# The row tiles of the pairs transposed by VectorE and five transfers instead of by TensorE

## The chip, the cores and the metric

One Trainium2 chip (trn2), one NeuronCore of it. The metric is the device time of one execution in microseconds. The engines are called PE (TensorE; PEld is its weight load), DVE (VectorE), ACT (ScalarE), POOL (GpSimd) and SP (SyncE, which here only issues transfers). Each engine works through its own list of instructions in order; semaphores make one wait for another.

## The reference

The input x has 2048 rows of 1024 numbers, in fp32 as everything here. A first layer is a linear map whose weight is a product of two matrices under a sparse mask, then gelu, the residual sum and a LayerNorm. A second layer is a linear map whose weights are looked up from packed codes in a table of 16 entries (or of 256, where a row's norm is over 64, which the kernel checks and leaves to a general path that isn't run here), again with residual sum and LayerNorm.

```python
def _L0_attn_ref(x, w1, w2, b2, sparse_mask):
    attn = jnp.einsum('ds,td->st', w1, w2) * sparse_mask
    y = jnp.einsum('bds,st->bdt', x, attn) + b2
    return jax.nn.gelu(y, approximate=False)

def _L0_ffn_ref(x, qweight, lut4, lut8, bias):
    e = jnp.linalg.norm(x, axis=-1) * LIN_SLOPE + LIN_INTER
    mask = e > EST_T
    w_l = dequant_kbit(qweight, lut4, B_L)
    w_h = dequant_kbit(qweight, lut8, B_H)
    y_l = jnp.einsum('bsi,oi->bso', x, w_l)
    y_h = jnp.einsum('bsi,oi->bso', x, w_h)
    y = jnp.where(mask[..., None], y_h, y_l) + bias
    return y

x = _layernorm(x + _L0_attn_ref(x, ...), axis=-1)
x = _layernorm(x + _L0_ffn_ref(x, ...), axis=-1)
```

## The kernel before

The rows are cut into 16 tiles of 128 (`NT`), each kept in SBUF as `x_tiles[n]` of 128x1024. PE contracts over partitions, so every row tile has to be there transposed, as 8 blocks of 128x128, before it can be multiplied.

First the two weights are made: `attn`, the masked product, as a band (L416, L423), and `wT`, the table weights, which the generator behind `steps()` unpacks piece by piece on DVE, POOL and ACT (L273 to L314) and PE transposes. The identity is added to `wT`, so the residual of the second layer is in the product.

Then the list `todo` (L625 to L632) is worked off. An entry "attention" transposes a tile on PE (`transpose_columns`, L258, copied from PSUM by ACT in L259), multiplies it with the band (L462), and goes through bias (DVE L477), gelu (ACT L478), residual sum (DVE L480) and LayerNorm. "left" and "right" are the two halves of 512 columns of the second layer for the tiles 0 to 5 (`EARLY` of them); the transposed tile is kept in the buffers `early0` to `early5` between the two. `ffn_half` ends in `combine` (DVE L502), and for the right half in `finish_rows`. A LayerNorm is: `nm` from the row sum (DVE L346), the sum of squares (ACT L349), the inverse root (POOL L351, L352) and `normalize` (DVE L356), into `o` and a transfer out for the second layer. The last twelve entries alternate right 0, attention 10, right 1, attention 11 and so on to right 5, attention 15. Two PSUM tiles `mm` of two banks each take turns, so a right half waits for the `combine` of the right half before, and an attention sum for the `z` read (L477) of the attention before.

The tiles 6 to 15 are done as five pairs. `pair_inputs` and `ffn_pair` multiply a pair's two row tiles as a 2x2 block product with seven products instead of eight, on sums of blocks: `weight_sums` makes t1 to t4 of the weights once (DVE L539 to L542), `pair_inputs` makes the blocks a11, a12, a22 and the sums s1 to s4 of a pair's transposed rows. A product is four matmuls of 128x128 by 128x512 (`times`, L582). PSUM holds u (twice), v and w for it, in the banks that `mm` had. Between the products DVE empties the sums: y11 (L595), y22 (L597), y12 (L599), then four `combine`, of which the last of each tile leads to `finish_rows`.

In `pair_inputs` PE makes four groups of four transposes (L556); a group takes every eighth column of its tile, as `wT` has them in that order. ACT copies three groups out of PSUM (L563, L564, L569), DVE makes s1 and s3 (L566, L567) reading the PSUM group of a21, and POOL makes s2 and s4 (L568, L570). Its results lie in `early0` to `early5` again, three of them for each pair, with two sets taking turns, and in `a22`. `pair_inputs` of the next pair is called ahead of `ffn_pair` of this one (L681 to L686), so its transposes stand in PE's list just ahead of this pair's products. A tile scheduler puts the instructions of each engine into an order by its own estimate, keeping dependences; so the order in the program text isn't quite the order on the engines. `count_odd` (L611) counts the rows that would need the general path, behind the first pair.

Of the kernel before, what the change touches and what calls it, by code (L numbers as in the profile page):

```python
# [9 lines left out]
FP = mybir.dt.float32  # L10
# [4 lines left out]
ALU = mybir.AluOpType  # L15
AX = mybir.AxisListType

P = 128
D = 1024
SOON = 12  # L20
PAIR = 2
KT = D // P
HALF = 512
# [4 lines left out]
WORDS = D // 32  # L28
BAND = 70
WIN = P + 2 * BAND  # L30
EARLY = 6
AHEAD = 2


def window(s):

    return max(0, s * P - BAND), min(D, (s + 1) * P + BAND)
# [153 lines left out]
def kernel(  # L191
# [13 lines left out]
    nc = tc.nc  # L205
    x = x.flatten_outer_dims()
    out = out.flatten_outer_dims()
    NT = x.shape[0] // P
# [4 lines left out]
    with ExitStack() as main:  # L213
        const = main.enter_context(tc.tile_pool(name="const", bufs=1))
        ps_tr = main.enter_context(tc.tile_pool(name="ps_tr", bufs=4, space=bass.MemoryType.PSUM))
# [5 lines left out]
        dq = first_sb.enter_context(tc.tile_pool(name="dq", bufs=1, side="right"))  # L221
        xp0 = main.enter_context(tc.tile_pool(name="xp0", bufs=1))
        work = main.enter_context(tc.tile_pool(name="work", bufs=1))


        q = dq.tile([P, KT, B_L, WORDS], I32, name="q")
# [11 lines left out]
        ident = const.tile([P, P], FP, name="ident")  # L238
# [119 lines left out]
        x_tiles = []  # L358
# [5 lines left out]

        attn = band.tile([P, KT, WIN], FP, name="attn")


        with tc.tile_pool(name="prod", bufs=1) as prod:
# [8 lines left out]
            def load_w1(first, n):  # L377
# [32 lines left out]
            for s in range(KT):  # L410
# [88 lines left out]

        def combine(n, h, ps, other):  # L500

            nc.vector.scalar_tensor_tensor(  # L502
                x_tiles[n][:, ts(h, HALF)],
                ps,
                1.0,
                other,
                ALU.mult,
                ALU.add,
                accum_out=sums[:, n, h : h + 1],
            )  # L510
# [20 lines left out]
        KH = KT // 2  # L531
# [10 lines left out]
            nc.vector.tensor_tensor(t4, b21, t2, ALU.subtract)  # L542
            return t1, t2, t3, t4

        def pair_inputs(pool, n):


            def halves(tag):
                both = late.tile([P, KT, P], FP, tag=tag, name="halves")
                return both[:, :KH, :], both[:, KH:, :]  # L550

            def transposes(m, half):
                cols = x_tiles[m].rearrange("t (b s) -> t s b", s=8)
                pt = ps_tr.tile([P, HALF // P, P], FP, tag="tr", name="pt")
                for k in range(KH):
                    nc.tensor.transpose(pt[:, k, :], cols[:, half * KH + k, :], ident)  # L556
                return pt


            side = n // PAIR % 2  # L560
            (a11, a12), (s1, s2), (s3, s4) = (halves(f"early{2 * i + side}") for i in range(3))
            a22 = pool.tile([P, KH, P], FP, tag="a22", name="a22", bufs=2)
            nc.scalar.copy(a11, transposes(n, 0))  # L563
            nc.scalar.copy(a22, transposes(n + 1, 1))  # L564
            a21 = transposes(n + 1, 0)
            nc.vector.tensor_tensor(s1, a21, a22, ALU.add)  # L566
            nc.vector.tensor_tensor(s3, a11, a21, ALU.subtract)  # L567
            nc.gpsimd.tensor_tensor(s2, s1, a11, ALU.subtract)  # L568
            nc.scalar.copy(a12, transposes(n, 1))  # L569
            nc.gpsimd.tensor_tensor(s4, a12, s2, ALU.subtract)  # L570
            return a11, a12, a22, s1, s2, s3, s4

        def ffn_pair(pool, n, blocks, weights):
            a11, a12, a22, s1, s2, s3, s4 = blocks
            t1, t2, t3, t4 = weights
            u = pool.tile([P, HALF], FP, tag="u", name="u", bufs=2)
            v = pool.tile([P, HALF], FP, tag="v", name="v", bufs=1)
            w = pool.tile([P, HALF], FP, tag="w", name="w", bufs=1)

            def times(ps, a, b, start, stop):  # L580
                for k in range(KH):
                    nc.tensor.matmul(  # L582
                        out=ps,
                        lhsT=a[:, k, :],
                        rhs=b[:, k, :],
                        start=start and k == 0,
                        stop=stop and k == KH - 1,
                        skip_group_check=True,
                    )

            left, right = bias_bc[:, :HALF], bias_bc[:, HALF:]
            y11, y12 = x_tiles[n][:, :HALF], x_tiles[n][:, HALF:]
            y22 = x_tiles[n + 1][:, HALF:]
            times(u, a11, b11, True, False)
            nc.vector.tensor_tensor(y11, u, left, ALU.add)  # L595
            times(w, s1, t1, True, False)
            nc.vector.tensor_tensor(y22, w, right, ALU.add)  # L597
            times(u, s2, t2, False, False)
            nc.vector.tensor_tensor(y12, u, right, ALU.add)  # L599
            times(w, s4, b22, False, True)  # L600
            combine(n, 1, w, y12)
            times(u, s3, t3, False, False)
            combine(n + 1, 1, u, y22)
            times(v, a12, b21, True, True)
            combine(n, 0, v, y11)
            finish_rows(n)
            times(u, a22, t4, False, True)
            combine(n + 1, 0, u, left)
            finish_rows(n + 1)
# [15 lines left out]
        todo = [("attention", n) for n in range(4)]  # L625
        for m in range(EARLY):
            todo.append(("left", m))
            if m < 4:
                todo.append(("attention", 4 + m))
        todo += [("attention", 8), ("attention", 9)]  # L630
        for m in range(EARLY):
            todo += [("right", m), ("attention", 10 + m)]  # L632
        unpack_after = [("attention", 1), ("left", 0), ("attention", 4), ("left", 1)]
        unpack_after += [("attention", 6), ("left", 2), ("left", 3), ("left", 4)]

        kept = {}

        def prepare(what, n):
            if what == "attention":
                return transposed(n, "xT", 2, False)  # L640
            if what == "left":
                kept[n] = transposed(n, f"early{n}", 1, True)
            return kept[n]
# [3 lines left out]
        for i, (what, n) in enumerate(todo):  # L647
            if (what, n) == ("right", 0):
                steps(100)
                transpose_pending(0)  # L650
                first_sb.close()
                last = main.enter_context(tc.tile_pool(name="last", bufs=1, side="right"))
                for m in range(SOON, NT):
                    load_x(last, m)
            if (what, n) == ("left", 0):
                transpose_pending(0)
            xT = ready
            if i + 1 < len(todo):
                ready = prepare(*todo[i + 1])
            if what == "attention":  # L660
                attention(n, xT)
                if n > 8 and checks < KT:
                    check_outside(checks)
                    checks += 1
            else:
                ffn_half(n, xT, 0 if what == "left" else 1)
                if what == "left" and n > 1:
                    check_outside(checks)
                    checks += 1
                if (what, n) == ("right", 0):  # L670
                    weights = weight_sums(last)
            if (what, n) in unpack_after:
                steps(1)
        while checks < KT:
            check_outside(checks)
            checks += 1
        first_ps.close()
        ps_pair = main.enter_context(
            tc.tile_pool(name="ps_pair", bufs=1, space=bass.MemoryType.PSUM)
        )  # L680
        blocks = pair_inputs(last, EARLY)  # L681
        for n in range(EARLY, NT, PAIR):
            now = blocks
            if n + PAIR < NT:
                blocks = pair_inputs(last, n + PAIR)
            ffn_pair(ps_pair, n, now, weights)  # L686
            if n == EARLY:
                count_odd()

# [41 lines left out]
```

## Time and profile before

| | |
|---|---|
| median of 3 runs | 384.45 us (384.4 to 384.62) |
| the profiled execution | 384.95 us, span 383.2 us, mean PE clock 0.981 |
| PE busy | 341.1 us (89%) |
| DVE, ACT, POOL busy | 213.0, 149.0, 120.7 us |
| a matmul of the pairs (L582) | 592 ns a record, 8 records (4 matmuls) for a product |
| a transpose of the pairs (L556) | x80, 10.1 us busy, 279 ns |
| s1, s3 on DVE (L566, L567) | 690 and 678 ns |
| s2, s4 on POOL (L568, L570) | 1275 and 1439 ns |
| normalize into o (DVE L356) | 988 ns mean |
| a 512 KB transfer out | 2.6 us from issue to landing |

The profile is of one execution. Its span runs from the first to the last instruction; the execution's own time is 1.75 us longer. A group of instructions is given as line, engine, operation, what is written and read, and count. "[idle before <-X]" says how long the engine stood idle just ahead of an instruction and what ended that. The chain that ended last is followed back from the last instruction, at each step to what released it. Matmul records of PE overlap by their pipelining, so their starts say more than their sums.

### The profile page before, as it was taken

To read this page: it belongs to the slowest core of one execution; us is meant where nothing else is said; L and a number is where in the kernel's file an instruction comes from. 1 tells how busy PE (TensorE), PEld (TensorE's weight loads), DVE (VectorE), ACT (ScalarE), POOL (GpSimd) and SP (SyncE) were. 2 spreads that over 40 slices of the span, in tenths; PEclk is the share of its full clock that TensorE was granted. 3 is DMA by queue.
4 is the path that set the end of the run, shared out by engine and by line. 5 is a ranking of instruction groups with operands and counts; after the bars stand their busy time and mean duration, and the time that the engine had idled before them with its cause. 6 is when DMAs were issued, how large, how long until landed. Compare 5 with 4: busy or idle time off the path is not lost.

```text
span 383.2 us, 3726 instructions
## 1 busy us (share of the span) xinstructions
PE 341.1 (89%) x1306; PEld 213.3 (56%) x1306; DVE 213.0 (56%) x334; ACT 149.0 (39%) x233; POOL 120.7 (31%) x144
## 2 busy tenths in 40 slices
PE   3699775979989889979999999899999999999990
PEld 3587565875666465665566665534544545444430
DVE  2698798988968893059544355642521614314221
ACT  0952843986395366152355533600401203002011
POOL 1991871875274611012022212530400301201000
PEclk9999998989999999999999999999999999999995
DMA  9999005800010111034121211100110201101102
GB/s 223 350 353 301 37 3 196 352 2 0 0 46 1 40 41 42 0 120 142 65 86 66 76 55 55 56 0 1 55 56 0 109 0 54 57 0 57 52 3 115
DMA packets 19705, 31.31 MB, mean 82 GB/s; under 512 B 6624, under 2 KB 13536, under 8 KB 19680
## 3 DMA queue, kind: packets, MB, share of 16 engines
q1 hardware_dynamic: 14416, 30.41, 21.8%
q10 hardware_dynamic: 5264, 0.59, 1.1%
q8 instruction: 12, 0.20, 0.2%
q14 instruction: 13, 0.11, 0.1%
HBM read 22.61 MB, written 8.39 MB: 81 GB/s over the span
## 4 chain that ended last, share of the span: by engine, by line
PE 38%; DVE 26%; POOL 14%; ACT 10%; issue 7%; DMA 3%; ACTq 0%; POOLq 0%; DVEq 0%; SPq 0%
PE u L582 16%; PE w L582 8%; ACT junk L349 6%; POOL root L302 5%; PE v L582 4%; PE mm L490 4%; DVE root L307 4%; PE mm L462 3%; DVE x L480 3%; DVE root L306 3%; POOL r L352 3%; DVE root L311 3%; POOL e L302 2%; DVE e L305 2%; DVE z L477 2%
## 5 line engine op out<-in xcount | busy, mean ns | idle before, releaser
L349 ACT ACTIVATE junk<-x,nm 128x1024 bf16<-128x1024 f32 x32 | 36.8, 1150 | 140.5 <-DVE nm L346 140.5
L490 PE MATMUL mm<-wT,xT 128*128 128x512 f32 x192 | 84.8, 594 | 5.6 <-DVE x L502 2.7
L351 POOL TENSOR_SCALAR r<-ss 128x1 f32<-128x1 f32 x32 | 9.9, 310 | 203.1 <-ACT junk L349 202.6
L462 PE MATMUL mm<-attn,xT 128*128 128x198 f32 (+2 forms) x320 | 62.5, 352 | 5.3 <-ACT xT L259 5.3
L462 PEld LDWEIGHTS mm<-attn,xT 128*128 128x128 f32 x320 | 54.8, 197 | 13.7 <-ACT xT L259 5.7
L490 PEld LDWEIGHTS mm<-wT,xT 128*128 128x128 f32 x192 | 35.5, 190 | 46.8 <-issue 39.5
L298 ACT ACTIVATE e<-v,lt,diff 128x1024 f32<-128x1024 uint8 x32 | 38.3, 1242 | 11.9 <-DVE v L273 10.3
L302 POOL TENSOR_SCALAR root<-v,diff,lt 128x1024 f32<-128x1024 uint8 x16 | 38.9, 2434 | 8.1 <-DVE root L311 7.4
L302 POOL TENSOR_SCALAR e<-v,diff,lt 128x1024 f32<-128x1024 uint8 x16 | 28.7, 1795 | 28.6 <-DVE v L273 25.6
L582 PE MATMUL u<-t,halves 128*128 128x512 f32 x80 | 36.0, 593 | 0.9 <-DVE x L595 0.9
L356 DVE TENSOR_SCALAR o<-x,nm,r 128x1024 f32<-128x1024 f32 x16 | 15.8, 988 | 35.1 <-POOL r L352 35.1
L416 PE MATMUL mm<-w2T,w_sb 128*128 128x268 f32 (+1 forms) x128 | 29.5, 384 | 4.6 <-issue 2.8
L478 ACT ACTIVATE z<-z 128x1024 f32<-128x1024 f32 x16 | 16.9, 1055 | 32.0 <-DVE z L477 32.0
L259 ACT COPY xT<-pt 128x512 f32<-128x512 f32 x44 | 23.4, 581 | 14.9 <-PE pt L258 9.6
L416 PEld LDWEIGHTS mm<-w2T,w_sb 128*128 128x128 f32 x128 | 23.8, 196 | 8.7 <-issue 3.2
L258 PE MATMUL pt<-ident,x 128*128 128x128 f32 x176 | 23.7, 280 | 4.1 <-DVE x L356 2.3
L356 DVE TENSOR_SCALAR x<-x,nm,r 128x1024 f32<-128x1024 f32 x16 | 13.0, 813 | 25.5 <-POOL r L352 23.2
L306 DVE COPY_PREDICATED root<-v,e 128x1024 f32<-128x1024 uint8 x16 | 22.7, 1419 | 7.8 <-POOL root L302 7.8
L582 PEld LDWEIGHTS u<-t,halves 128*128 128x128 f32 x80 | 15.1, 190 | 20.4 <-issue 18.7
L305 DVE COPY_PREDICATED e<-v,e 128x1024 f32<-128x1024 uint8 x16 | 24.4, 1534 | 3.4 <-ACT e L298 3.4
L258 PEld LDWEIGHTS pt<-ident,x 128*128 128x128 f32 x176 | 21.5, 155 | 7.4 <-DVE x L356 2.6
L307 DVE COPY_PREDICATED root<-v,e 128x1024 f32<-128x1024 uint8 x16 | 25.4, 1590 | 0.1
(76 smaller groups left out, 398.7 us busy)
## 6 DMA issues: line engine op xcount, KB each, us to landing
x<-in_L_attn_x_dram SPq DMA_DIRECT2D x16, 512.0 KB, 6.6
out_dram<-o SPq DMA_DIRECT2D x16, 512.0 KB, 2.6
w_raw<-in_L_attn_w_dram SPq DMA_DIRECT2D x8, 512.0 KB, 5.8
w_sb<-in_L_attn_w_dram SPq DMA_DIRECT2D x3, 1024.0 KB, 7.7
w_sb<-in_L_attn_w_dram SPq DMA_DIRECT2D x2, 512.0 KB, 4.7
raw<-_L_attn_sparse_mask_dram SPq DMA_DIRECT2D x2, 413.0 KB, 3.0
mask<-_L_attn_sparse_mask_dram SPq DMA_DIRECT2D x6, 134.0 KB, 7.1
raw<-_L_attn_sparse_mask_dram SPq DMA_DIRECT2D x2, 349.0 KB, 3.0
```

The costliest lines, as they stand in the source:

```text
L258: nc.tensor.transpose(pt[:, j, :], block(g * (HALF // P) + j), ident)
L298: nc.scalar.activation(entry[j], plane(0), AF.Identity, scale=d_k, bias=l_k)
L302: nc.gpsimd.tensor_scalar(entry[j], plane(0), d_k, l_k, ALU.mult, ALU.add)
L305: nc.vector.copy_predicated(entry[2], plane(1), entry[3])
L306: nc.vector.copy_predicated(root, plane(1), entry[1])
L307: nc.vector.copy_predicated(root, plane(2), entry[2])
L349: nc.scalar.activation(junk, u, AF.Square, bias=nm, accum_out=ss)
L356: nc.vector.tensor_scalar(dst, u, nm, r, ALU.add, ALU.mult)
L416: nc.tensor.matmul(out=ps[:, : hi - lo], lhsT=w1_sb[s][:, k, :], rhs=w2T[:, k, lo:hi], start=(k == 0), stop=(k == KT - 1),)
L462: nc.tensor.matmul(out=ps[:, a:b], lhsT=xT[:, s, :], rhs=attn[:, s, a - lo : b - lo], start=h not in fresh, stop=hi == D or (h == 0 and wi ...
L490: nc.tensor.matmul(out=ps, lhsT=xT[:, k, :], rhs=wT[:, k, ts(h, HALF)], start=(k == 0), stop=(k == KT - 1),)
L582: nc.tensor.matmul(out=ps, lhsT=a[:, k, :], rhs=b[:, k, :], start=start and k == 0, stop=stop and k == KH - 1, skip_group_check=True,)
```

## The change

The PE transposes of the pairs go. A new helper, `squares`, transposes a row tile in two steps. DVE's transpose turns each 32x32 square of the tile within itself: of the 1024 columns, read as four blocks c of 32 columns j by 8 positions k, the square (c, k) for each group of 32 rows is turned, and lands in the tile `squares`. The squares are then put where the transposed tile has them by way of DRAM: one transfer of 512 KB writes `squares` to a DRAM tile `there`, and four transfers of 128 KB read it back, each into 32 partitions of the tile `rows`, in pieces of 1 KB. All five are issued by SP.

`pair_inputs` now gets the two `rows` tiles of a pair. ACT copies the first tile whole into a1 (a11 and a12), and half of the second into a22; DVE makes s1 and s3 from `rows`; POOL makes s2 and s4 as before. The set of `early` buffers for a pair is the other one of the two than before.

The work is tied to fixed steps of DVE. For the pairs behind the first, `ffn_pair` calls `between` with the instructions that write y11, y22 and the `combine` of y12; `squares` of the next pair's first tile is issued after the first of these, of its second tile after the second, and its `pair_inputs` after the third (`tc.issue_after`). For the first pair, tiles 6 and 7, the three calls stand behind right 3, right 4 and right 5 in the text.

In the order that results, PE's list is the same as before up to the pairs and has no transposes from there on. On DVE the transposes of tiles 6 and 7 stand in the stretch of attention 8 and 9, ahead of the weight sums; s1 of the first pair stands behind right 2's `combine`, s3 behind right 4's, and right 1's `combine` stands ahead of attention 10's `normalize` instead of behind it. In the pairs DVE has y11, the `normalize` of the pair before, a transpose, y22, a transpose, y12; s1 and s3 of the next pair stand behind this pair's last `combine`. On SP the two writes and eight reads of a pair stand between the outputs of the pair before and its own.

```diff
@@ squares, new; pair_inputs @@
+        def squares(pool, n):
+            t = pool.tile([P, Q, KT, SQ], FP, tag="squares", name="squares", bufs=2)
+            nc.vector.transpose(
+                out=t, in_=x_tiles[n].rearrange("t (c j k) -> t c k j", c=Q, k=KT)
+            )
+            there = moved.tile([Q, SQ, Q, KT * SQ], FP, tag="there", name="there", bufs=4)
+            nc.sync.dma_start(
+                out=there.rearrange("a j c e -> (a j) (c e)"),
+                in_=t.rearrange("p c k r -> p (c k r)"),
+            )
+            rows = pool.tile([P, Q, KT, SQ], FP, tag="rows", name="rows", bufs=2)
+            for c in range(Q):
+                nc.sync.dma_start(
+                    out=rows[ts(c, SQ), :, :, :].rearrange("j a k r -> j a (k r)"),
+                    in_=there[:, :, c, :].rearrange("a j e -> j a e"),
+                )
+            return rows.rearrange("p a k r -> p k a r")
+
-        def pair_inputs(pool, n):
+        def pair_inputs(pool, n, top, low):
...
-            def transposes(m, half):
-                cols = x_tiles[m].rearrange("t (b s) -> t s b", s=8)
-                pt = ps_tr.tile([P, HALF // P, P], FP, tag="tr", name="pt")
-                for k in range(KH):
-                    nc.tensor.transpose(pt[:, k, :], cols[:, half * KH + k, :], ident)
-                return pt
...
-            side = n // PAIR % 2
+            side = (n - EARLY) // PAIR % 2
...
-            nc.scalar.copy(a11, transposes(n, 0))
-            nc.scalar.copy(a22, transposes(n + 1, 1))
-            a21 = transposes(n + 1, 0)
-            nc.vector.tensor_tensor(s1, a21, a22, ALU.add)
-            nc.vector.tensor_tensor(s3, a11, a21, ALU.subtract)
+            nc.scalar.copy(by_squares(a1), top)
+            nc.vector.tensor_tensor(by_squares(s1), low[:, :KH], low[:, KH:], ALU.add)
+            nc.vector.tensor_tensor(by_squares(s3), top[:, :KH], low[:, :KH], ALU.subtract)
+            nc.scalar.copy(by_squares(a22), low[:, KH:])
             nc.gpsimd.tensor_tensor(s2, s1, a11, ALU.subtract)
-            nc.scalar.copy(a12, transposes(n, 1))
             nc.gpsimd.tensor_tensor(s4, a12, s2, ALU.subtract)
@@ ffn_pair @@
-            nc.vector.tensor_tensor(y11, u, left, ALU.add)
+            between(0, nc.vector.tensor_tensor(y11, u, left, ALU.add))
...
-            nc.vector.tensor_tensor(y22, w, right, ALU.add)
+            between(1, nc.vector.tensor_tensor(y22, w, right, ALU.add))
...
-            combine(n, 1, w, y12)
+            between(2, combine(n, 1, w, y12))
@@ main @@
+        def prepare_pair(n, part):
+            if n == NT:
+                return
+            if part < PAIR:
+                rows[n + part] = squares(last, n + part)
+            else:
+                blocks[n] = pair_inputs(last, n, rows[n], rows[n + 1])
...
+            if what == "right" and n >= EARLY - 3:
+                prepare_pair(EARLY, n - (EARLY - 3))
...
-        blocks = pair_inputs(last, EARLY)
         for n in range(EARLY, NT, PAIR):
-            now = blocks
-            if n + PAIR < NT:
-                blocks = pair_inputs(last, n + PAIR)
-            ffn_pair(ps_pair, n, now, weights)
+            def between(part, done, m=n + PAIR):
+                with tc.issue_after(done.ins):
+                    prepare_pair(m, part)
+            ffn_pair(ps_pair, n, blocks[n], weights, between)
```

More of the change, by code (lines that the diff above doesn't have):

```diff
@@ L30 @@
 WIN = P + 2 * BAND
+SQ = 32
+Q = P // SQ
 EARLY = 6
@@ L223 @@
         work = main.enter_context(tc.tile_pool(name="work", bufs=1))
+        moved = main.enter_context(
+            tc.tile_pool(name="moved", bufs=1, space=bass.MemoryType.DRAM)
+        )
         q = dq.tile([P, KT, B_L, WORDS], I32, name="q")
@@ L500, in combine @@
         def combine(n, h, ps, other):
-            nc.vector.scalar_tensor_tensor(
+            return nc.vector.scalar_tensor_tensor(
                 x_tiles[n][:, ts(h, HALF)],
@@ L543, in weight_sums @@
             return t1, t2, t3, t4
-        def pair_inputs(pool, n):
+        def squares(pool, n):
[13 more added lines that the diff above has]
+                    in_=there[:, :, c, :].rearrange("a j e -> j a e"),
+                )
+            return rows.rearrange("p a k r -> p k a r")
@@ L548, in halves @@
+        def pair_inputs(pool, n, top, low):
             def halves(tag):
                 both = late.tile([P, KT, P], FP, tag=tag, name="halves")
-                return both[:, :KH, :], both[:, KH:, :]
-            def transposes(m, half):
-                cols = x_tiles[m].rearrange("t (b s) -> t s b", s=8)
-                pt = ps_tr.tile([P, HALF // P, P], FP, tag="tr", name="pt")
-                for k in range(KH):
-                    nc.tensor.transpose(pt[:, k, :], cols[:, half * KH + k, :], ident)
-                return pt
@@ L560, in pair_inputs @@
-            side = n // PAIR % 2
-            (a11, a12), (s1, s2), (s3, s4) = (halves(f"early{2 * i + side}") for i in range(3))
-            a22 = pool.tile([P, KH, P], FP, tag="a22", name="a22", bufs=2)
-            nc.scalar.copy(a11, transposes(n, 0))
-            nc.scalar.copy(a22, transposes(n + 1, 1))
-            a21 = transposes(n + 1, 0)
-            nc.vector.tensor_tensor(s1, a21, a22, ALU.add)
-            nc.vector.tensor_tensor(s3, a11, a21, ALU.subtract)
+                return both, both[:, :KH, :], both[:, KH:, :]
@@ new lines, in by_squares @@
+            def by_squares(block):
+                return block.rearrange("p k (a r) -> p k a r", a=Q)
+            side = (n - EARLY) // PAIR % 2
+            (a1, a11, a12), (_, s1, s2), (_, s3, s4) = (
+                halves(f"early{2 * i + side}") for i in range(3)
+            )
+            a22 = pool.tile([P, KH, P], FP, tag="a22", name="a22", bufs=2)
+            nc.scalar.copy(by_squares(a1), top)
+            nc.vector.tensor_tensor(by_squares(s1), low[:, :KH], low[:, KH:], ALU.add)
@@ L568, in pair_inputs, with ffn_pair @@
+            nc.vector.tensor_tensor(by_squares(s3), top[:, :KH], low[:, :KH], ALU.subtract)
+            nc.scalar.copy(by_squares(a22), low[:, KH:])
             nc.gpsimd.tensor_tensor(s2, s1, a11, ALU.subtract)
-            nc.scalar.copy(a12, transposes(n, 1))
             nc.gpsimd.tensor_tensor(s4, a12, s2, ALU.subtract)
             return a11, a12, a22, s1, s2, s3, s4
-        def ffn_pair(pool, n, blocks, weights):
+        def ffn_pair(pool, n, blocks, weights, between):
             a11, a12, a22, s1, s2, s3, s4 = blocks
@@ L636 @@
         kept = {}
+        rows, blocks = {}, {}
+        def prepare_pair(n, part):
[5 more added lines that the diff above has]
+                blocks[n] = pair_inputs(last, n, rows[n], rows[n + 1])
         def prepare(what, n):
```

## The prediction

> **What bounds the kernel now.** I read the page first (span 383.2 us, PE busy 89%), then the chain that ended last from 268 us on, since the diff touches the pairs. In the chain (start us, us, what), the change's target stands three times, each between two runs of matmuls without a gap:
>
> ```profile
> 267.71 3.00 PE u L582 x7
> 270.83 2.12 PE pt L556 x16
> 272.96 3.44 PE u L582 x8
> ...
> 293.56 3.43 PE u L582 x8
> 296.99 1.77 PE pt L556 x16
> 298.76 3.44 PE u L582 x8
> ...
> 319.37 3.43 PE u L582 x8
> 322.80 1.79 PE pt L556 x16
> 324.59 3.44 PE u L582 x8
> ```
>
> So from 253 us PE alone sets the pace: a pair is seven products of 3.43 us, 24.03 us, and the 16 transposes for the next but one stand openly on PE. They are 2.12, 1.77 and 1.79 us, 16 each. The other 32 of the 80 transposes lie before 253 us, so I read PE's timeline there (start, us, engine, instruction, [idle before <- releaser]):
>
> ```profile
> 236.20 3.76 PE L462 MATMUL mm<-attn,xT 128*128 128x198 f32 x20
> 239.80 2.92 PE L556 MATMUL pt<-ident,x 128*128 128x128 f32 x24
> 243.94 1.13 PE L582 MATMUL u<-wT,halves 128*128 128x512 f32 x2 [1.23 <-DVE z L477]
> ```
>
> Here the transposes fill a hole. The first pair's product takes the bank of the last attention sum, and waits until VectorE has read it (z L477). VectorE is late for that:
>
> ```profile
> 241.94 0.81 DVE L356 TENSOR_SCALAR o<-x,nm,r 128x1024 f32<-128x1024 f32 x1 [2.31 <-POOL r L352]
> 242.67 1.22 DVE L477 TENSOR_TENSOR z<-mm,b_bc 128x1024 f32<-128x1024 f32 x1
> ```
>
> z ends at 243.89 and PE starts at 243.94. From 180 to 240 us PE is gapless with 11.34 us a step (195.32, 206.66, 218.00 for the right halves). VectorE's own serial chain of two LayerNorms a step is 10.91 us (combine 194.21, 205.12). So there VectorE is nearly level, with under 1 us to spare at each right half.
>
> **What the skill says.** "VectorE: DVE Perf Modes", The three transpose paths: VectorE transposes only within 32x32 blocks, 311 ns for 128x128 bf16, about a cycle per element. "Vector Engine (DVE) Microarchitecture Reference", 3.8, says the same: one element per cycle per lane. No run here shows the operation. "SBUF — State Buffer", Door 1: The DMA port swizzle: reads that change the 16-byte line at every element pay a penalty; the new transposes read with 32-byte steps. The trace has one such operand (ident in L314, 128 columns): 0.39 us, where the contiguous 128x198 of L423 takes 0.34, so a step of 32 bytes may cost up to a cycle per element more. "TensorE: Matmul & The Clock Gate", Part 1: after an idle window of about 3.4 us PE's clock is halved until it was busy for about 3.4 us. The trace agrees. Rows of a stretch: us, busy of the five engines, granted clock, DMA share, GB/s.
>
> ```profile
> 58.00:61.50 3.50, 0.00 (x0) 0.00 (x0) 3.50 (x5) 0.57 (x2) 0.00 (x0) 0.98 0.00 0
> 61.50:63.00 1.50, 1.43 (x4) 1.33 (x5) 1.47 (x2) 1.48 (x4) 0.00 (x0) 0.50 0.74 251
> 63.00:65.00 2.00, 2.00 (x8) 1.67 (x7) 1.97 (x9) 0.00 (x0) 0.00 (x0) 0.55 0.99 365
> 65.00:67.00 2.00, 2.00 (x14) 1.83 (x14) 0.37 (x2) 1.60 (x2) 1.46 (x2) 1.00 0.95 367
> ```
>
> After a gap of 4.74 us the band product took 5.44 us instead of 3.76: 1.7 us lost. The gaps of 1.2 to 2.5 us after 140 us left the clock at 1.00.
>
> **The change, part by part.**
>
> *Removed:* 80 PE transposes (10.1 us busy), and 15 ACT copies of 128x512 (8.7 us); five of 128x1024 (about 1.05 us each, as L478) and five of 128x512 take their place, in ACT's idle time. On the path: 1.77 + 1.79 after pair 8 began, the rest up to there (below).
>
> *Added on VectorE:* ten transposes of 128x1024. Lower bound 1.15 us, the cycle-per-element time (128x1024 with one PSUM operand: 1.22); with the stride penalty 2.3 us; at four cycles per element 4.4. I take 1.2, since a transpose has one source and 3.8 promises the rate, and keep 2.3 and 4.4. The sums s1 and s3 stay at 0.68.
>
> *Added on SP:* per tile one 512 KB write, which lands after 2.6 us as the output does, then four 128 KB reads, each behind that landing, about 3 us like the mask loads of 29 to 413 KB (2.2 to 3.0), and 0.35 us of issue each.
>
> *Stage before the pairs.* Tile 6's transpose falls into VectorE's idle time from 168.7 to 171.0 (it waits for PE's last wT transposes, about 169): free up to 2.0 us. Tile 7's stands between x+z (L480) and nm of attention 9: all 1.15 us are late. So right 0's combine goes from 181.23 to 182.4; its bank is wanted at 183.98, no stall. From there one order moves in favour: right 1's combine now precedes attention 10's normalize, in its wait, and hides 0.9 us. o of right 1 comes 0.3 late. s1 stands behind right 2's combine (+0.61, o at 209.4 instead of 208.5) and s3 behind right 4's (+0.61). Right 3's combine ends at 218.3 against the wanted 218.0: PE 0.3 late. At the end z of attention 15 finishes at 243.89 + 1.5 = 245.4. SP's row reads are issued among the check loads at 171 to 193 us; their users, ACT's two copies at 187 and 199, find them landed.
>
> *The hole.* PE ends attention 15 at 240.3 and starts pair 6 at 245.45. It is now empty for 5.1 us, longer than the 4.74 above: I charge 1.7 us of half clock. s1 to s4 are ready, and y11, y22, y12 keep ahead of their products (y22 ends near 255, wanted 257.4). The 1.2 us that odd (L614) took beside a GpSimd product shrinks to 0.2. Pair 6 ends at 245.45 + 24.03 + 1.7 = 271.2, and pair 8 starts at 271.3 instead of 272.96: 1.65 gained.
>
> *A pair (T its start).* VectorE: combine to T+1.4, s1 to 2.1, s3 to 2.8, total and nm; ACT square and GpSimd s2, s4, r; y11 at 3.7 to 4.4; o to 6.3; transpose to 7.5; y22 7.5 to 8.2 (its bank wanted at 10.3); transpose to 9.4; y12 10.5 to 11.2 (wanted 13.7). s1 is wanted at 3.43, s2 at 6.9. On SP the second tile is written at 9.5, landed 12.5, its reads issued to 14, landed 17; the output DMAs come at 6 and 24, so nothing queues. First use: ACT's copy for T+24. Slack 7 us. No stall: 24.03.
>
> *Sum.* 271.3 + 4 x 24.03 = 367.4 (before 372.66), then the same tail of 10.54: span 378.0 against 383.2, 5.2 less. The profiled execution took 384.95, 1.75 more than its span; the median of the runs is 384.45. So 384.45 - 5.2 = **379.2 us**.
>
> **Rivals.**
>
> *The stride costs.* 2.3 us a transpose: 0.3 + 1.1 later before the pairs, nothing in them (slack to 3.0): 380.6. For it: L314; against: only one of its operands and eight short rows.
>
> *The hole doesn't slow the clock,* since the windows run free: 377.5. For: 2.5 us at 170 were harmless. Against: 2.28 us at 76 did halve it (0.50).
>
> *Slower: VectorE becomes the bound.* In a pair y12 ends at T + 7.7 + 2d for a transpose of d; beyond 13.7, d = 3.0, each further us of d stalls PE by 2 us in four pairs, and before the pairs it adds twice. The gain of 5.2 is gone at about d = 3.2. At 4.4: 2.4 + 3.2 before the pairs, 4 x 2.8 in them: 396. For it: nothing shows an fp32 transpose's rate. Against: 3.8's rate.
>
> *The round trip is late.* Reads of 1 KB pieces into 32 rows need 10 us instead of 3: then s1 and the copy come late, by some us a pair: 383 to 388. Against: DMA share 0.06 to 0.11 in the pairs.
>
> **How the numbers follow.** Main case 0.50 (own range 378.2 to 380.3), stride 0.20, no half clock 0.12, VectorE the bound 0.09, late round trip 0.06 (half of it slower), better than all 0.03. Predicted is the main case. From 377.0 to 382.5 about 0.83 are held; the upper end reaches past the stride case. A difference under 0.2% (0.8 us) can't be told from none. Faster 0.85, within 0.03, slower 0.12.
>
> **What would show it.** Right: no 128x128 transposes on PE after 240 us; VectorE's transposes at 1.1 to 1.3 us; pairs spaced 24.0; a PE gap of about 5 us behind the last attention with clock 0.5 after it. Wrong: a transpose over 3 us, y12 or y22 as PE's releaser within a pair, ACT's copy of rows waiting for DMA with PE behind it, or right halves spaced over 11.5 us.

## The result, and the profile after

The changed kernel takes 380.54 us (median of 4 runs, 380.22 to 381.81) where the kernel before took 384.53 beside it: ratio 0.9901, 95% interval 0.9875 to 0.9926. Run again beside later experiments it took 380.90 (5 runs, 380.60 to 382.03), ratio 0.9907, 0.9892 to 0.9921. So 3.6 to 4.0 us are gained (by ratios, by medians); 5.2 were forecast, in a range that holds the result. The profiled execution took 380.86 us, its span 379.1, so again 1.76 lies outside the span.

The chain that ended last, after the change (start us, us, what), from the first pair on:

```profile
244.41 1.14 DVE z L482
245.55 0.04 issue
245.60 5.92 PE u L604 x8
251.52 3.43 PE w L604 x8
...
268.69 3.43 PE u L604 x8
272.12 0.12 PE pc L642 x2
272.24 3.63 PE u L604 x8
275.87 3.43 PE w L604 x8
```

No transposes stand between products any more. Pairs 8, 10, 12 and 14 start at 272.17, 296.31, 320.34 and 344.38: 24.03 to 24.14 us each, as forecast. But the first product takes 5.92 us instead of 3.4 to 3.6, and what the chain shows ahead of it is VectorE. PE's and VectorE's timelines there (start, us, engine, instruction, [idle before <- releaser]):

```profile
237.21 3.76 PE L467 MATMUL mm<-attn,xT 128*128 128x198 f32 x20
245.60 5.92 PE L604 MATMUL u<-wT,halves 128*128 128x512 f32 x8 [4.63 <-DVE z L482]
```

```profile
241.14 0.15 DVE L351 TENSOR_SCALAR nm<-total 128x1 f32<-128x1 f32 x1
243.60 0.81 DVE L361 TENSOR_SCALAR o<-x,nm,r 128x1024 f32<-128x1024 f32 x1 [2.30 <-POOL r L357]
244.32 1.22 DVE L482 TENSOR_TENSOR z<-mm,b_bc 128x1024 f32<-128x1024 f32 x1
```

PE is empty from 240.97 to 245.60, where the kernel before did 32 transposes. VectorE stands idle for 2.30 us of that time, waiting for GpSimd's r, with the `z` that PE needs queued behind. Then PE runs at half clock. Stretches of this profile (us, busy of PE, PEld, DVE, ACT, POOL, granted clock, DMA share, GB/s):

```profile
240.00:242.00 2.00, 0.97 (x5) 0.57 (x3) 1.23 (x5) 0.59 (x1) 0.35 (x1) 1.00 0.00 0
...
244.00:246.00 2.00, 0.40 (x1) 0.40 (x2) 1.54 (x2) 0.42 (x1) 0.00 (x0) 0.50 0.38 158
...
248.00:250.00 2.00, 2.00 (x3) 0.67 (x2) 0.09 (x1) 1.24 (x2) 0.38 (x2) 0.50 0.00 0
250.00:252.00 2.00, 2.00 (x6) 0.99 (x5) 0.44 (x1) 0.00 (x0) 0.74 (x3) 0.97 0.00 0
```

VectorE's new transposes, in its list of groups (count | busy us, mean ns | idle before):

```profile
L554 DVE STREAM_TRANSPOSE squares<-x 128x1024 f32<-128x1024 f32 x10 | 20.2, 2024 | 0.5 <-PE pt L263 0.5
```

They take 2.02 us, not the 1.2 that I had taken.

The theory for the experiments: the change is worth all of PE's 80 transposes wherever PE is the limit, but ahead of pair 6 it only empties a hole whose end VectorE sets, and there some of the gain is given back through the halved clock. The rivals: the transpose's own length on VectorE is what costs the rest; the round trip through DRAM does; the slow first product has another cause than the gap.

### The profile page after: what moved, and what is told of

Same layout as the page of the kernel before. It is cut to its first block, busy times and chain, and to the rows that moved or that the text cites. A ratio compares the mean times of both kernels' runs of the same rounds, so it can differ in the third digit from the quotient of the medians.

```text
span 379.1 us, 3687 instructions
## 1 busy us (share of the span) xinstructions
PE 336.0 (89%) x1226; PEld 206.7 (55%) x1226; DVE 231.2 (61%) x344; ACT 149.2 (39%) x228; POOL 119.9 (32%) x144
## 4 chain that ended last, share of the span: by engine, by line
PE 42%; DVE 26%; POOL 12%; ACT 9%; issue 8%; DMA 1%; ACTq 0%; POOLq 0%; DVEq 0%
PE u L604 18%; PE w L604 9%; ACT junk L354 5%; PE mm L467 5%; PE v L604 5%; POOL root L307 4%; PE mm L495 4%; DVE root L312 3%; DVE x L485 3%; DVE root L311 3%; POOL r L357 3%; DVE z L482 3%; POOL e L307 2%; DVE e L310 2%; DVE root L316 2%
## 5 line engine op out<-in xcount | busy, mean ns | idle before, releaser
L495 PE MATMUL mm<-wT,xT 128*128 128x512 f32 x192 | 86.2, 602 | 5.4 <-DVE x L507 2.7
L467 PE MATMUL mm<-attn,xT 128*128 128x198 f32 (+2 forms) x320 | 63.9, 358 | 5.3 <-ACT xT L264 5.3
L467 PEld LDWEIGHTS mm<-attn,xT 128*128 128x128 f32 x320 | 56.1, 201 | 13.7 <-ACT xT L264 5.7
L307 POOL TENSOR_SCALAR root<-v,diff,lt 128x1024 f32<-128x1024 uint8 x16 | 36.4, 2277 | 8.2 <-DVE root L316 7.4
L307 POOL TENSOR_SCALAR e<-v,diff,lt 128x1024 f32<-128x1024 uint8 x16 | 29.6, 1852 | 28.5 <-DVE v L278 25.5
L361 DVE TENSOR_SCALAR o<-x,nm,r 128x1024 f32<-128x1024 f32 x16 | 13.0, 812 | 34.4 <-POOL r L357 34.4
L311 DVE COPY_PREDICATED root<-v,e 128x1024 f32<-128x1024 uint8 x16 | 22.9, 1433 | 7.8 <-POOL root L307 7.8
L485 DVE SCALAR_TENSOR_TENSOR x<-z,x 128x1024 f32<-128x1024 f32 x16 | 20.4, 1276 | 9.2 <-ACT z L483 9.2
L586 ACT COPY halves<-rows 128x1024 f32<-128x1024 f32 x5 | 5.2, 1042 | 51.2 <-DMA rows<-there 39.0
```

The costliest lines, as they stand in the source:

```text
L307: nc.gpsimd.tensor_scalar(entry[j], plane(0), d_k, l_k, ALU.mult, ALU.add)
L311: nc.vector.copy_predicated(root, plane(1), entry[1])
L361: nc.vector.tensor_scalar(dst, u, nm, r, ALU.add, ALU.mult)
L467: nc.tensor.matmul(out=ps[:, a:b], lhsT=xT[:, s, :], rhs=attn[:, s, a - lo : b - lo], start=h not in fresh, stop=hi == D or (h == 0 and wi ...
L485: nc.vector.scalar_tensor_tensor(xt, z, 1.0, xt, ALU.mult, ALU.add, accum_out=total)
L495: nc.tensor.matmul(out=ps, lhsT=xT[:, k, :], rhs=wT[:, k, ts(h, HALF)], start=(k == 0), stop=(k == KT - 1),)
```

## The experiments

### The new way only for pairs 10, 12 and 14

```diff
+            if n <= 8:
+                return                      # in prepare_pair: no squares for pairs 6 and 8
...
-            if what == "right" and n >= EARLY - 3:
+            if False:
                 prepare_pair(EARLY, n - (EARLY - 3))
...
+        blocks[EARLY] = by_tensor(last, EARLY)              # as pair_inputs was before
+        blocks[EARLY + PAIR] = by_tensor(last, EARLY + PAIR)
```

> Pairs 6 and 8 get their blocks by TensorE's transposes as in the kernel before (32 transposes in the hole, none by VectorE before 245 us); only pairs 10, 12 and 14 take the new way. Theory: up to pair 8 it is the kernel before without the 2.12 us that stood open for pair 10, then 1.77 and 1.79 us fewer: pair 8 starts at 270.8, span 377.5, time 384.5 - 5.7 = 378.8 us, so 1.7 under the changed kernel: the new way was worth nothing for pairs 6 and 8. Rival (the changed kernel's gain came from all 80 transposes evenly): three fifths of the 4.0 us gained stay, 382.1.

Measured: 379.81 us, ratio 0.9860 (0.9845 to 0.9874). That is below the changed kernel's interval (0.9892 to 0.9921): by the ratios 0.47% or 1.8 us, by the medians alone 0.7 to 1.1; forecast were 1.7. PE's timeline of it:

```profile
241.57 2.85 PE L603 MATMUL pt<-ident,x 128*128 128x128 f32 x24
244.29 1.12 PE L629 MATMUL u<-wT,halves 128*128 128x512 f32 x2
...
271.09 3.70 PE L629 MATMUL u<-wT,halves 128*128 128x512 f32 x8
```

The hole is full again, the clock stays at 1.00, and pair 8 starts 1.1 us earlier than in the changed kernel, though it now pays 32 transposes on PE. So for the first two pairs the new way is worth less than nothing; what the change gains, it gains in the other three.

### Keeping PE busy in the hole

```diff
+        for _ in range(6):                  # second version: range(10)
+            warm = ps_tr.tile([P, HALF // P, P], FP, tag="tr", name="warm")
+            for j in range(HALF // P):
+                nc.tensor.transpose(warm[:, j, :], ident, ident)
         for n in range(EARLY, NT, PAIR):
```

> 24 transposes of ident (results unused) are put on TensorE into the empty 4.63 us ahead of the first product of pair 6. Theory (the hole, now empty, halves the clock and so gives back part of the gain): with some 2.9 us of work in it the first product takes 3.6 us instead of 5.92, pair 8 starts at 269.9 instead of 272.17, time 378.2 us (380.5 - 2.3). Rival (the 5.92 us came from something else than the gap, such as the throttle's own swings or a wait inside the product): first product still near 5.9, time 380.5. Rival (VectorE's longer transposes set the rest): 380.5 too.

Measured: 381.61 us (380.07 to 382.02), ratio 0.9909 (0.9891 to 0.9927): no gain, so this forecast failed. The 24 transposes ran at once and left 2.88 us empty, and the clock was halved all the same (first product 5.40 us). Besides, the order that the scheduler made of VectorE's work was another one: y11 of pair 8 came 0.62 us late for PE. So the same edit with 40:

> 40 transposes of ident instead of 24 in the hole: in the run with 24 they were done 2.9 us ahead of z's end, and the clock was at 0.50 all the same (first product 5.40 us). 40 take some 4.6 us and leave a gap of about 1.0 us. Theory (a gap of 2.9 us or more halves the clock, one of 1 us doesn't): first product 3.6 us, pair 8 at 270.0 instead of 271.85, time 379.6 us (381.6 - 2.0). Rival (not the gap but something else in this place slows the clock): first product over 5 us, 381.6.

Measured: 380.15 us (379.48 to 380.68), ratio 0.9878 (0.9863 to 0.9893). PE's timeline of the two, first with 24, then with 40:

```profile
240.14 2.78 PE L718 MATMUL warm<-ident 128*128 128x128 f32 x24
245.80 5.40 PE L604 MATMUL u<-wT,halves 128*128 128x512 f32 x8 [2.88 <-DVE z L482]
...
271.85 3.70 PE L604 MATMUL u<-wT,halves 128*128 128x512 f32 x8
```

```profile
241.64 4.53 PE L718 MATMUL warm<-ident 128*128 128x128 f32 x40
246.27 3.70 PE L604 MATMUL u<-wT,halves 128*128 128x512 f32 x8
...
270.62 3.70 PE L604 MATMUL u<-wT,halves 128*128 128x512 f32 x8
```

With the gap filled, the first product takes 3.70 us, and from its start to that of pair 8 24.35 us pass, against 26.05 with the gap of 2.88 and 26.57 in the changed kernel. So it is the gap that slows this product, and it costs about 2 us. Of that 1.2 to 1.5 us show in the time against the version with 24 (by ratios, by medians; 2.0 forecast); in this profile attention 15 had ended 1.5 us later than in that one. The late y11 of pair 8 is in this version too (0.63 us), so the two compare evenly, but against the changed kernel both carry it: pair 8 takes 25.0 us in both, where it takes 24.14 in the changed kernel.

### The first product without the wait for z, in both kernels

```diff
-            u = pool.tile([P, HALF], FP, tag="u", name="u", bufs=2)
+            if n == EARLY:
+                u = ps_tr.tile([P, HALF], FP, tag="tr", name="u")
+            else:
+                u = pool.tile([P, HALF], FP, tag="u", name="u", bufs=2)
```

In the changed kernel:

> The changed kernel with one edit: u of pair 6 lies in a bank of the transposes' pool instead of the bank of attention 15, so the first product needn't wait for z (L482). Theory (the hole ahead of pair 6 takes the gain, and VectorE has room after it): first product starts at 241.0 with 3.6 us, y11 is taken at 248.6 and y22 at 252.6, which costs TensorE 0.7 + 0.5 us, pair 8 starts at 266.2 instead of 272.17, time 374.5 us. Rival (VectorE is the bound there and its lateness only moves into the pair): TensorE waits for y11 and y22 for 3 to 5 us, time 378 to 380.

Measured: 376.10 us (376.00 to 376.57), ratio 0.9773 (0.9760 to 0.9786). In the kernel before:

> The kernel before with the same edit (u of pair 6 in a bank of the transposes' pool). Theory: its hole was filled by 3.7 us of transposes, so only the waits of 0.9 us around them go: 383.6 us. Against the changed kernel with that edit (374.5) the change is then worth 9.1 us, close to the 10.1 us of all 80 transposes, where it was worth 4.0 with the hole. Rival (the hole has nothing to do with what the change is worth): this kernel gains as much by the edit as the changed one, 378.5, and the difference stays 4.0.

Measured: 385.38 us (21 runs), ratio 1.0012 (1.0006 to 1.0019). PE's timelines, of the changed kernel with the edit and of the kernel before with it:

```profile
241.02 3.60 PE L607 MATMUL u<-wT,halves 128*128 128x512 f32 x8
245.99 3.70 PE L607 MATMUL w<-t,halves 128*128 128x512 f32 x8 [1.38 <-DVE z L482]
...
267.32 3.70 PE L607 MATMUL u<-wT,halves 128*128 128x512 f32 x8
```

```profile
244.24 1.13 PE L585 MATMUL w<-t,halves 128*128 128x512 f32 x2 [0.46 <-DVE halves L566]
...
246.09 3.60 PE L585 MATMUL u<-wT,halves 128*128 128x512 f32 x8
249.52 2.74 PE L585 MATMUL w<-t,halves 128*128 128x512 f32 x6
253.00 3.67 PE L585 MATMUL u<-t,halves 128*128 128x512 f32 x8 [0.74 <-DVE x L598]
...
272.88 3.60 PE L585 MATMUL u<-wT,halves 128*128 128x512 f32 x8
```

The same edit is worth 4.4 to 5.2 us in the changed kernel (by medians, by ratios) and less than nothing in the kernel before. There the 32 transposes fill the time anyway, and the scheduler put one matmul of w ahead of u (244.24). The third product still waits for y11 (L598), which VectorE takes behind the last normalize, 0.74 us where it was 0.94 without the edit: pair 8 starts at 272.88, as it did without it (272.79). So the change is worth 2.39% or 9.2 us between these two kernels (forecast 9.1), close to the 10.1 us of all 80 transposes, against 3.6 to 4.0 with the hole. The sizes of both forecasts were off: 376.1 instead of 374.5, since w too lay in a bank of attention 15 and waited 1.38 us; and 385.4 instead of 383.6, since I had not followed y11 in the kernel before.

### The transpose's source

```diff
-                out=t, in_=x_tiles[n].rearrange("t (c j k) -> t c k j", c=Q, k=KT)
+                out=t, in_=x_tiles[n].rearrange("t (c k j) -> t c k j", c=Q, k=KT)
```

> VectorE's transpose reads its source in contiguous runs of 32 elements instead of steps of 32 bytes; each 32x32 square then holds other columns, so pairs compute with columns in another order and the output is not the reference's. Theory A (the 2.02 us are the step's price over one element per cycle): 1.15 to 1.25 us a transpose. Theory B (it is the rate of an fp32 transpose whatever the source): 2.0 us again. Time: the end of z(15) is 0.1 to 0.9 us earlier under A, 379.6 to 380.4 us; the same as the changed kernel under B, 380.5.

Measured: 380.58 us (380.32 to 381.98), ratio 0.9907 (0.9888 to 0.9926). The group of the transposes, with contiguous source:

```profile
L554 DVE STREAM_TRANSPOSE squares<-x 128x1024 f32<-128x1024 f32 x10 | 12.4, 1236 | 0.5 <-PE pt L263 0.5
```

Theory A holds: 1.24 us without the step, 2.02 with it. The step of 32 bytes costs 0.79 us per 128x1024. But 7.9 us less work on VectorE leave the time where it was. In this profile z ended at 244.72, 0.8 us earlier than 245.54, as Theory A has it. But the gap was 5.22 instead of 4.63 us, the first product took 6.00, and pair 8 started at 271.42, 0.75 us earlier; the medians of the runs show none of it. So the transpose's length was at most a small part of what the change lost.

### Each transpose of the pairs done twice

```diff
-            nc.vector.transpose(
+            for _ in range(1 if n < EARLY + PAIR else 2):
+                nc.vector.transpose(
...
```

> Each of the eight transposes made within pairs is done twice, so a transpose costs VectorE 4.04 us there; the two of pair 6 stay single. Theory (the prediction's slack: no stall up to d = 3.0, then 2 us per us of d in each of four pairs): y12 late by 2.1 us a pair, TensorE waiting for it, 380.5 + 8.3 = 388.8 us. Rival (VectorE is idle for long enough in a pair to take it): under 382. Rival (it has no slack at 2.02): 8 x 2.02 = 16 us, 396.

Measured: 388.76 us (388.34 to 390.17), ratio 1.0120 (1.0100 to 1.0140), within 0.1 us of the forecast. PE's timeline in pair 10 and the start of pair 12:

```profile
299.04 3.60 PE L605 MATMUL u<-wT,halves 128*128 128x512 f32 x8
...
310.38 3.67 PE L605 MATMUL w<-wT,halves 128*128 128x512 f32 x8 [0.88 <-DVE x L620]
314.85 3.70 PE L605 MATMUL u<-t,halves 128*128 128x512 f32 x8 [0.80 <-DVE x L622]
...
325.25 3.60 PE L605 MATMUL u<-wT,halves 128*128 128x512 f32 x8
```

The pair takes 26.21 us, 2.2 more than 24.03, and the releasers are y22 (L620) and y12 (L622), as the prediction's slower rival had it. The loss is not even over the four pairs, as the forecast took it: in pair 6 TensorE waits 0.38 us only, pair 8 takes 27.23 us, 3.2 more than 24.03, and pairs 10 and 12 lose 2.2 and 2.3. That the sum is met within 0.1 us is in part luck. So in a pair VectorE has room for one transpose of 2.02 us per tile and not for one of 4.04; the prediction's edge of 3.0 us fits both.

### A longer way through DRAM

```diff
+            for hop in range(2 if n >= EARLY + PAIR else 0):
+                nxt = moved.tile([Q, SQ, Q, KT * SQ], FP, tag=f"hop{hop}", name="nxt", bufs=4)
+                nc.sync.dma_start(out=nxt.rearrange("a j c e -> (a j) (c e)"),
+                                  in_=there.rearrange("a j c e -> (a j) (c e)"))
+                there = nxt
```

> The way of each tile of pairs 8 to 14 through DRAM is made longer by two copies of its 512 KB from DRAM to DRAM, one behind the other, between the write and the four reads; the order of TensorE's products follows (v ahead of w from pair 8 on). Theory (the transfers have some 7 us of slack in a pair, so they are not what sets the time): at 3 us a copy the rows land some 6 us later and TensorE waits under 0.5 us a pair, 380.5 to 382 us. Rival (the round trip is near its limit): 3 us or more a pair, 390 or above.

Measured: 394.90 us (393.85 to 395.55), ratio 1.0260 (1.0241 to 1.0278): this forecast failed. At pair 8, ACT's copy of the first tile's rows in the changed kernel, then with the longer way the transfers on SP, this copy, and PE behind it:

```profile
264.32 1.05 ACT L586 COPY halves<-rows 128x1024 f32<-128x1024 f32 x1 [14.88 <-DMA rows<-there]
```

```profile
258.96 2.98 SPq L564 DMA_DIRECT2D nxt<-there  x2
263.19 2.84 SPq L564 DMA_DIRECT2D nxt<-nxt  x2
268.32 4.01 SPq L571 DMA_DIRECT2D rows<-nxt  x8
```

```profile
273.51 1.04 ACT L593 COPY halves<-rows 128x1024 f32<-128x1024 f32 x1 [1.56 <-DMA rows<-nxt]
```

```profile
274.61 3.70 PE L611 MATMUL u<-wT,halves 128*128 128x512 f32 x8 [1.58 <-ACT halves L593]
```

In the changed kernel this copy runs at 264.32 to 265.37, when its rows land, and PE wants it at 272.17: 6.8 us of slack, where I had worked out 7. Here it starts at 273.51, 9.2 us later instead of the 6 that two copies of 3 us make: the first tile's two copies took 4.2 and 5.1 us from issue to landing, and its reads were issued (268.32) as the second one had landed. 9.2 less 6.8, less the 0.8 us by which pair 8 was due later in this execution, is 1.6, the wait seen.

From pair 10 on, more is lost (27.6 to 27.7 us for pairs 10 and 12). The second tile's last copy, issued at 295.43, landed after 4.1 us, but its reads stand on SP behind an output transfer, which waits for VectorE's normalize,

```profile
300.73 0.36 SPq L524 DMA_DIRECT2D out_dram<-o  x1
301.19 2.13 SPq L571 DMA_DIRECT2D rows<-nxt  x4
```

and its copy on ACT, at 306.75, waited 3.70 us for them. PE waits 1.4 to 1.5 us a pair for s1, which VectorE makes of these rows, and 1.62 us for a combine of VectorE, in the order that the scheduler made for the longer way. How much of the 14 us is transfer and how much is that order, this run doesn't part. It confirms the slack of about 7 us at pair 8, and in this run more was lost past that than the excess.

### VectorE's order ahead of pair 6

```diff
-            nc.vector.tensor_tensor(z, ps, b2_bc, ALU.add)
+            added = nc.vector.tensor_tensor(z, ps, b2_bc, ALU.add)
+            if n == NT - 1:
+                with tc.issue_after(added.ins):
+                    late_write.pop()()      # o and its transfer, of right 5
...
+            if n == EARLY - 1:                  # in finish_rows; write() is o and its transfer
+                late_write.append(write)
+            else:
+                write()
```

> The changed kernel with its banks as they are and one order changed on VectorE: z of attention 15 (L482), for which TensorE waits with the first product of pair 6, goes ahead of the normalize that writes o of right 5 (L361), in whose 2.3 us of waiting for GpSimd's r it fits. Theory (the hole is VectorE's order, not its load): z ends 1.6 us after attention 15's last matmul, the gap is 1.7 us instead of 4.63 and leaves the clock at 1.00, the first product takes 3.6 us, pair 8 starts at 266.9 instead of 272.17, 375.2 us. Rival (the lateness is VectorE's load and moves on into the pair): TensorE waits for y11 and y22 for the same 3 us or more, 378 to 380.5.

Measured: 376.64 us (375.65 to 377.77), ratio 0.9789 (0.9772 to 0.9805). Two more runs give pair 6 new banks and put the last normalize of tile 15 later, the first without the new order of z, the second with it. The edit for both:

```diff
+            if n == EARLY:                          # and u as above
+                w = ps_tr.tile([P, HALF], FP, tag="tr", name="w")
...
-            normalize(xt, xt, nm, r)
+            if n == NT - 1:
+                last_norm.append(lambda: normalize(xt, xt, nm, r))
+            else:
+                normalize(xt, xt, nm, r)
...
+            if n == EARLY:
+                with tc.issue_after(second.ins):    # second: y22 of pair 6
+                    last_norm.pop()()
```

Banks and late normalize without the new order of z:

> The changed kernel with u and w of pair 6 in banks of the transposes' pool, and the last normalize (tile 15, wanted only by pair 14) put behind y22 of pair 6. In the run with u alone moved, TensorE still waited 1.38 us for z, since w lay in the bank of attention 15, and 0.17 us for y22. Theory (the hole's cost is that of the banks): first product at 241.0, second at 244.5 without a wait, third at 248.9 behind y11 (1.0 us), none at y22, pair 8 at 266.2 against 267.3 with u alone: 375.0 us, 1.1 under the 376.1 of that run. Rival (VectorE is already the bound in pair 6): the wait moves to y11 and y22, 376.1 as with u alone.

Measured: 376.33 us (376.12 to 376.76), ratio 0.9786 (0.9772 to 0.9799). All together:

> That order together with u and w of pair 6 in banks of the transposes' pool and tile 15's normalize behind y22. Theory: no gap and no wait from attention 15 to pair 8; y11 is taken at 245.8 where it was 248.6, y22 before 250; pair 8 starts at 265.3 instead of 266.7 (banks and late normalize alone), 374.9 us against 376.3. Rival (what the banks alone left is not a wait of TensorE): 376.3.

Measured: **374.40 us** (373.42 to 374.98), ratio 0.9727 (0.9712 to 0.9742), the fastest of all: 6.5 us below the changed kernel's 380.90 beside it. PE's timelines, of the new order alone and of all together:

```profile
242.74 5.40 PE L616 MATMUL u<-wT,halves 128*128 128x512 f32 x8 [2.40 <-DVE z L482]
...
268.79 3.70 PE L616 MATMUL u<-wT,halves 128*128 128x512 f32 x8
```

```profile
237.94 3.76 PE L467 MATMUL mm<-attn,xT 128*128 128x198 f32 x20
241.53 3.60 PE L627 MATMUL u<-wT,halves 128*128 128x512 f32 x8
244.97 3.60 PE L627 MATMUL w<-t,halves 128*128 128x512 f32 x8
...
265.78 3.70 PE L627 MATMUL u<-wT,halves 128*128 128x512 f32 x8
```

With `z` put into VectorE's 2.30 us of waiting, the hole shrinks by half with no work taken away, so the hole was order more than load. But 2.40 us were left where I had forecast 1.7, and the clock was halved behind them: 376.6 instead of 375.2. In that run z still stands behind an earlier wait of VectorE for GpSimd's r, with the normalize of attention 14:

```profile
239.73 0.81 DVE L361 TENSOR_SCALAR x<-x,nm,r 128x1024 f32<-128x1024 f32 x1 [2.30 <-POOL r L357]
...
241.46 1.23 DVE L482 TENSOR_TENSOR z<-mm,b_bc 128x1024 f32<-128x1024 f32 x1
```

With all together PE goes from attention 15 into pair 6 and to pair 8 without a gap. The banks and the late normalize alone brought pair 8 to 266.74, 0.6 us earlier than u alone (1.1 forecast), and no less time: PE waited 0.60 us ahead of the third product and 0.23 us for y22. In the profiled execution the last output took 4.3 us from issue to landing, where it took 3.3 in the one with u alone, which more than uses up the 0.6 us; why it took longer stays open. Of these edits only the bank of u was also tried in the kernel before, so whether the new order of z or the late normalize would gain there too is not shown.

### The changed kernel once more

> The changed kernel as it is, beside the others on one chip: 380.5 us as before; pair 8 starts at 272.2 if the gap ahead of pair 6 halves the clock in this execution too.

Measured: 380.90 us, as given above. In its profile the first product took 5.50 us behind a gap of 5.51, and pair 8 started at 272.14.

## Why the prediction was right, and where it was off

**The removed transposes.** Right. The 1.77 and 1.79 us between pairs 8, 10 and 12 are gone, and no wait took their place. That only the ones standing in the open count is shown by the hybrid (pairs 6 and 8 worth nothing) and by the two kernels without the hole (9.2 us).

**The transpose's duration: mis-sized.** I took 1.2 us and kept 2.3 for the stride; it is 2.02. Both numbers were near something measured: a contiguous source takes 1.24 us, and the step adds 0.79 to it (1.1 in the rival). The step that failed is the choice, by which the row L314 was set aside as "only one of its operands and eight short rows". The page on SBUF, at the place that the prediction cites, was to be believed here. The stride rival's forecast of 380.6 equals the result, but not by its mechanism: it had let the longer transposes cost 1.4 us before the pairs, and taking the step away brought the time no lower.

**The stage before the pairs.** Right within 0.2 us at its end: z of attention 15 ends at 245.54, forecast 245.4, though each transpose there was 0.8 longer. In part that is luck: with transposes of 1.24 us, near the 1.2 of the forecast, z ended at 244.72, so the sum was some 0.7 us too late and the longer transpose made up for it. Tile 6's was free, as worked out (168.77 to 170.83).

**The hole.** Right in kind: PE starts pair 6 at 245.60 (245.45 forecast) behind an empty stretch of 4.6 to 5.5 us (5.1), and the clock is halved. The price is the term that was mis-sized: 1.7 us taken from one earlier gap in one execution; 2.3 us here (5.92 against 3.60), 1.9 in the second execution. With this, pair 8 starts at 272.17 instead of 271.3, and that 0.9 us is most of the miss in the span (379.1 against 378.0). One gap in one execution could not give it: that same gap ahead of 61.5 us (4.41 to 4.74 us in all profiles) was followed by a band product of 5.26 to 6.75 us where 3.76 is the full clock's, so its price alone ran from 1.5 to 3.0 us. And where the prediction says of the page's 3.4 us that the trace agrees, it holds for the 4.74 us shown there, not for the 2.28 us at 76 that its own rival names.

**The pairs.** Right: 24.03 us, no stall, s1 to s4 in time. The slope beyond the edge (2 us per us and pair) held in the sum when the transposes were doubled, though not pair by pair. The slack of 7 us, worked out for a second tile, measured 6.8 at the first tile's copy for pair 8.

**What the prediction did not see.** It treated the hole's end as given. VectorE's place for `z`, behind a 2.30 us wait of its own, was in the profile of before, where the transposes hid it; that order, two PSUM banks and one late normalize were worth 6.5 us in the changed kernel.

## What to carry to other kernels

Work taken off the busiest engine is gained only where that engine is the limit: go through it place by place, and ask for each whether the work stood in the open or filled a wait for somebody else. Where it filled a wait, the next step is that wait, and here the order on one engine and the owner of two banks were worth more (6.5 us) than the change itself (3.6 to 4.0). TensorE, emptied this way, also came back at half clock here (1.7 to 2.6 us in the seven profiles that kept a gap of 2.40 us or more), so an edit that leaves a gap is not finished.

## What was not expected of the hardware

The Trainium skill ("TensorE: Matmul & The Clock Gate", Part 1) has the clock halved after an idle window of about 3.4 us. Here shorter gaps did it: 2.40 us (first product 5.40 us) and 2.88 us (5.40), while 1.38 us did not (3.70). Ahead of 78 us, nine profiles have a gap of 1.83 to 2.28 us, and in eight of them the clock went to 0.50 behind it; in the ninth (2.21 us, in the run of the doubled transposes) it stayed at 1.00, as it did behind the gaps of 1.31 to 1.61 us of the other five. And the gap of 2.53 or 2.54 us ahead of 172 us, which all fourteen profiles of this case have, was followed by a clock of 0.50 in eight of them and of 1.00 in the other six; the changed kernel, profiled twice, is among both (its product there took 8.54 us once and 7.13 once, and pair 8 started at 272.17 and 272.14 all the same). The price does not follow the gap's length either: 5.92 us behind 4.63, 5.50 behind 5.51.

A VectorE transpose of fp32 in 32x32 squares took 1.24 us per 128x1024 from a contiguous source and 2.02 us from one with steps of 32 bytes. That agrees with the Trainium skill ("SBUF — State Buffer", Door 1: The DMA port swizzle), by which each access that moves to another 16-byte line pays a penalty; the size, 0.79 us here, is from these runs.

The first tile's write to DRAM, which fell beside the x loads, took 9.2 us to land; the median of all ten was 3.0.
